# One stretch a round for the 64-wide matmuls of a two-layer graph network

## The chip, the cores and the metric

The kernel runs on one core of a Trainium2 chip. Its time is the device time of one execution in microseconds (us). The core has a matrix engine (PE, TensorE), whose results go to PSUM, eight banks of 128 partitions by 512 fp32; a vector engine (DVE), an activation engine (ACT) and GpSimd (POOL)[...]; and SP, which here issues nearly all DMA transfers. Each engine has its own queue of instructions and takes them in order; semaphores tie the queues together.

## What is computed

Sixty-four graphs of 256 nodes with 512 features pass through two layers, all in fp32. Layer 0 is attention with eight heads of 64 and a gate, layer 1 graph attention. Cut to what matters:

```python
h = relu(layernorm(x))                        # layer 0
q, k, v = h @ Wq.T, h @ Wk.T, h @ Wv.T         # 8 heads of 64
scores = where(adj != 0, q @ k.T / 8, -inf)    # per head
c = softmax(scores) @ v
gate = sigmoid(concat([c, h]) @ Wg.T + bg)
x = x + gate * h + (1 - gate) * c
h = relu(layernorm(x))                        # layer 1
Wh = h @ W
e = leaky_relu(Wh @ a1 + (Wh @ a2).T, 0.2)     # masked by adj
x = x + elu(softmax(e) @ Wh)
```

## The kernel before, in words

**Tiles.** A graph's 256 nodes are two tiles of 128 (NT = 2), its 512 features four chunks of 128 (HC = 4). Everything stays fp32. A matmul of fp32 stands in the trace as two instructions.

**Products by Strassen.** The four large products, qk (q and k together), v, z (the gate) and wh, are done in seven steps instead of eight (`strassen`, L158). Steps 1 and 2 write PSUM bank a, steps 6, 7 and 4 bank b, steps 5 and 3 bank c. Between them partial sums are taken out: u1, u2, u3, and the four blocks of the result, c00, c01, c10, c11. u1 and c00 are copies on ACT (L187), the others additions on DVE (L185). u2 and u3 read bank b between steps 6, 7 and 4, and c11 reads bank c between steps 5 and 3, so PE may not go on in a bank before DVE has read it. The order in which steps and sums are issued is written out by hand. The sums of input blocks that Strassen needs are made on POOL (`token_sums`, L146, instructions L152 to L155).

**Attention.** Heads come in two halves of four; a half has two pairs jj, a pair two heads i. `a_scores` (L328) multiplies 64 rows of q with 64 rows of k (L338, shape 64\*128: the two heads of a pair use the upper and lower half of the array at once) into four PSUM tiles `ps`, one for each head. `a_max` (L349) has DVE add the mask and find the row's extreme (L353), `a_exp` (L358) is the exponential on ACT (L362), `a_scale` (L367) multiplies by the reciprocal of the sum on POOL (L374), `a_turn` (L376) transposes 32x32 blocks on DVE (L383). `a_send` writes the blocks to DRAM and `a_fetch` (L401) reads them back in the transposed order, both on SP's queue. `a_weigh` (L407) multiplies with v (L415, shape 128\*64, again two at a time) into the tile `pc`, and `a_evac` copies that to cT on ACT (L425). All other matmuls use the whole array, shape 128\*128.

**The gate and layer 1.** z is the gate's product, `g_tanh` is on ACT, `g_mix` (L460) on DVE. The result is transposed and sent through DRAM (y), added to x (`g_residual`), normalised, transposed and sent again (h1), and multiplied into wh. `g_edges` transposes the edge column on PE (L554, tile `pe`), `g_logits`, `g_leaky`, `g_exp` are layer 1's attention, `g_out` its product (L613, tile `po`), and `g_neg`, `g_pos`, `g_elu`, `g_add` the final function and sum.

**Rounds.** `emit_round(i)` (L648) issues one round, for five graphs at once: p = i + 1 is projected (qk, v), i is in attention, q = i - 1 in its gate, r = i - 2 in layer 1's attention, o = i - 3 is stored. There is no scheduler: under a manual schedule each engine's queue has the order of the calls in `emit_round`. A round's matmuls before the change, in order: z(q), wh(r), scores of i's second half, weighings of its first half, `pe`, qk(p), v(p), output tile 0 of r, scores of p's first half, weighings of i's second half, output tile 1.

**The next h.** A graph's first normalised h goes the same way a round earlier: normalised on ACT (L213), transposed by blocks on DVE (`p_turn`, L239), sent to DRAM (`there_h`) and fetched (`p_fetch`, L269, tile `hT_l`) by SP, whose queue takes all these transfers in the order of the calls; `p_sums` makes its Strassen sums on POOL, and qk needs both.

**Buffers.** PSUM has one tile each for banks a, b and c and five tiles for everything else (tag w). In SBUF the pools that the change touches are qk (3 tiles) and e (4 tiles, for scores, for their blocks, and for the transposed blocks alike).

Of the kernel before, what the change touches and what calls it, by code (L numbers as in the profile page):

```python
# [22 lines left out]
def kernel(  # L23
# [44 lines left out]
    def pool(name, bufs, **kw):  # L68
# [2 lines left out]
    const = pool("const", 1)  # L71
    st = pool("st", 3)
    sb = {tag: pool(tag, bufs) for tag, bufs in {
        "x": 5, "adj": 1, "mask": 4, "hT": 3, "S": 3, "qk": 3, "v": 2, "wh": 1, "e": 4,
        "cT": 1, "z": 2, "h": 1, "tmp": 5, "U": 3,
    }.items()}
    ps = {tag: pool(f"ps_{tag}", bufs, space=bass.MemoryType.PSUM) for tag, bufs in {
# [250 lines left out]
    def a_scores(g, half):  # L328
        s = graphs[g]
        qk = s["qk"][half]  # L330
        psc = {}
        for jj in range(2):
            for i in range(2):
                psc[jj, i] = ps["w"].tile([P, NT, N], F32, tag="t", name=f"ps_{g}_{half}_{jj}_{i}")
            for t in range(NT):
                for i in range(2):
                    r = i * DK
                    nc.tensor.matmul(  # L338
                        psc[jj, i][:, t, :], qk[r:r + DK, 0, jj, t * P:(t + 1) * P], qk[r:r + DK, 1, jj, :],
                        start=True, stop=True,  # L340
                    )
        s["ps", half] = psc
        for jj in range(2):
            s["e", half, jj] = sb["e"].tile([P, 2, NT, N], F32, tag="t", name=f"e_{g}_{half}_{jj}")
        s["low", half], s["sums", half], s["rec", half] = (
            st.tile([P, 2, 2, NT], F32, tag=tag, name=f"{tag}_{g}_{half}") for tag in ("low", "sums", "rec")
        )
# [16 lines left out]
                accum_out=s["sums", half][:, jj, i, t:t + 1],  # L364
            )

    def a_scale(g, half, jj):  # L367
        s = graphs[g]
        rec = s["rec", half][:, jj]
        nc.vector.reciprocal(rec, s["sums", half][:, jj])  # L370
        for i in range(2):
            for t in range(NT):
                e = s["e", half, jj][:, i, t, :]
                nc.gpsimd.tensor_scalar(e, e, rec[:, i, t:t + 1], 1.0, ALU.mult, ALU.mult)  # L374

    def a_turn(g, half, jj, i):  # L376

# [29 lines left out]
    def a_weigh(g, half):  # L407
        s = graphs[g]
        eT = [s.pop(("eT", half, jj)) for jj in range(2)]
        pc = s["pc"] = ps["w"].tile([P, 2, N], F32, tag="t", name=f"pc_{g}_{half}")  # L410
        for jj in range(2):
            for kc in range(NT):
                for i in range(2):
                    hd = 4 * half + 2 * jj + i
                    nc.tensor.matmul(  # L415
                        pc[i * DK:(i + 1) * DK, jj, :].rearrange("p (t a c) -> p t a c", t=NT, c=32),
                        s["v"][:, kc, hd * DK:(hd + 1) * DK], eT[jj][:, i, kc],
                        start=(kc == 0), stop=(kc == NT - 1),
                    )
# [79 lines left out]
    def g_residual(g):  # L499
        s = graphs[g]  # L500
        for t in range(NT):
            x = s["x"][:, t, :]
            if g >= LAST:
                nc.vector.tensor_tensor(x, x, s["py"][t], ALU.add)
            else:
                x = x.rearrange("p (j i c) -> p j i c", i=4, c=32)
                nc.vector.tensor_tensor(x, x, s["yT"][:, :, t].rearrange("p i j c -> p j i c"), ALU.add)

    def g_stats(g, t):
        norm_stats(graphs[g], t, f"l1_{g}")  # L510
# [137 lines left out]
    def emit_round(i):  # L648


        p, q, r, o = i + 1, i - 1, i - 2, i - 3

        def do(fn, g, *args):
            if 0 <= g < B:
                fn(g, *args)

        def run(fn, g, steps):
            if 0 <= g < B:
                if (fn, g) not in products:
                    products[fn, g] = fn(g), set()  # L660
                product, done = products[fn, g]
                for step in steps.split():
                    if step not in done:
                        product(step)
                        done.add(step)


        run(g_gate, q, "1")
        do(g_neg, o, 1)
        do(p_turn, p)  # L670
        do(p_send, p)
        do(a_scale, i, 0, 0)
        do(a_exp, i, 0, 1, 0)
        do(a_exp, i, 0, 1, 1)
        run(g_gate, q, "u1 6 u2 5")
        do(a_scale, i, 0, 1)
        do(a_turn, i, 0, 0, 0)
        do(a_turn, i, 0, 0, 1)
        do(a_send, i, 0, 0)
        do(g_pos, o, 1)  # L680
        do(g_sums_h, r)
        run(g_gate, q, "7")
        do(a_turn, i, 0, 1, 0)
        do(a_turn, i, 0, 1, 1)
        do(a_send, i, 0, 1)
        do(p_fetch, p)
        do(a_fetch, i, 0, 0)
        do(g_diff, q)
        run(g_gate, q, "u3 c11")
        do(p_mask, p)  # L690
        chore(chores, 2)
        do(g_elu, o, 1)
        run(g_gate, q, "2 c00 4 c10")
        do(g_tanh, q, 0)
        do(a_fetch, i, 0, 1)
        run(g_gate, q, "3 c01")
        do(g_mix, q, 0, True)

        run(g_wh, r, "1 u1")
        do(g_tanh, q, 1)  # L700
        do(g_mix, q, 0, False)
        run(g_wh, r, "6 u2 5")
        do(g_mix, q, 1, True)
        run(g_wh, r, "7 u3")
        do(g_mix, q, 1, False)
        chore(chores, 2)
        run(g_wh, r, "c11 2 c00")
        do(p_sums, p)
        do(g_turn, q)
        do(g_send, q)  # L710
        run(g_wh, r, "4 c10 3 c01")
        do(a_scores, i, 1)
        if i > 0:
            do(a_weigh, i, 0)
        do(a_max, i, 1, 0)
        do(g_add, o, 0)
        do(g_add, o, 1)
        do(g_store, o)
        do(a_exp, i, 1, 0, 0)
        do(a_exp, i, 1, 0, 1)  # L720
        do(a_max, i, 1, 1)
        if i > 0:
            do(a_evac, i, 0)
        do(g_fetch, q)
        do(g_edges, r)
        do(a_exp, i, 1, 1, 0)
        do(g_logits, r)
        do(a_scale, i, 1, 0)
        do(g_leaky, r)
        if i == -1:  # L730
            chore(weight_sums("q"), 4)
            chore(weight_sums("k"), 4)
        run(p_qk, p, "1")
        do(a_exp, i, 1, 1, 1)
        do(g_exp, r)
        do(a_scale, i, 1, 1)
        if i == 0:
            run(p_qk, p, "u1 6 u2 5 7 u3 c11 2 c00 4 c10")
            a_weigh(i, 0)
            a_evac(i, 0)  # L740
        do(a_turn, i, 1, 0, 0)
        do(a_turn, i, 1, 0, 1)
        do(a_send, i, 1, 0)
        do(load_graph, p + 1)
        if i == -1:
            for key in ("gh", "gc", "1"):
                load_weight(key, nc.sync)
            load_small()
            chores.extend(weight_sums("gh") + weight_sums("gc"))
            chores.append(lambda: nc.vector.tensor_scalar_mul(hbg, hbg, 0.5))  # L750
            chores.extend(edge_columns() + weight_sums("1"))
        run(p_qk, p, "u1 6 u2 5")
        do(g_turn_e, r)
        do(g_send_e, r)
        do(g_rec, r)
        do(a_turn, i, 1, 1, 0)
        do(a_turn, i, 1, 1, 1)
        do(a_send, i, 1, 1)
        run(p_qk, p, "7 u3 c11")
        chore(chores, 1)  # L760
        do(a_fetch, i, 1, 0)
        do(g_fetch_e, r)
        do(a_fetch, i, 1, 1)
        do(g_residual, q)
        run(p_qk, p, "2 c00")
        do(g_stats, q, 0)
        run(p_qk, p, "4 c10")
        chore(chores, 1)
        do(g_stats, q, 1)
        do(g_root, q)  # L770
        run(p_qk, p, "3 c01")
        chore(chores, 1)
        if i == -1:
            chore(weight_sums("v"), 4)
        run(p_v, p, "1 u1")
        do(g_bias, q)
        do(g_norm, q)
        run(p_v, p, "6 u2 5")
        if q < LAST:
            do(g_turn_h, q)  # L780
            do(g_send_h, q)
        run(p_v, p, "7 u3 c11 2 c00")
        chore(chores, 1)
        do(p_stats, p + 1, 0)
        run(p_v, p, "4 c10")
        chore(chores, 1)
        do(p_stats, p + 1, 1)
        do(p_root, p + 1)
        run(p_v, p, "3 c01")
        chore(chores, 1)  # L790
        do(p_bias, p + 1)
# [63 lines left out]
```

## Time and profile before

| | |
|---|---|
| median of 3 runs | 3233.6 us (3232.44 to 3236.47) |
| profiled execution, its own time | 3231.35 us |
| its span from first to last instruction | 3229.6 us |
| granted clock of PE | 0.992 |
| busy: PE, DVE, POOL, ACT | 3169.3, 2526.9, 1716.3, 1304.5 us |
| DMA | 590.66 MB, mean 183 GB/s |

The profile is one execution on the chip. A busy time is the union of an engine's instructions; matmuls are pipelined and their recorded times overlap, so the distance between the starts of two matmuls tells more than how long each is. A line of the timeline has start, duration, engine, line of the kernel, operation, the tile written and the tiles read, shapes and a count; a bracket at its end tells how long the engine stood idle before it and what released it. `PEld` is the loading of weights into the array.

### The profile page before, as it was taken

What the parts mean: (1) busy time and instruction counts of PE and PEld (TensorE: products, weight loads), DVE (VectorE), ACT (ScalarE), POOL (GpSimd) and SP (SyncE); (2) the same over time, 40 slices, a digit from 0 to 9 for tenths busy, and PEclk for the clock granted to TensorE, in tenths of its full rate; (3) what the DMA queues carried; (4) which work ended last, traced back from release to release, by engine and by line L of the source; (5) the groups of instructions that cost most, each with busy time, mean ns of one, the idle gap of its engine ahead of it and who ended that gap; (6) DMA issues with size and microseconds to landing.
All of it is one profiled execution on the core that took longest, in us unless ns stands there. A gap on an engine that the chain in (4) does not pass through costs nothing.

```text
span 3229.6 us, 67257 instructions
## 1 busy us (share of the span) xinstructions
PE 3169.3 (98%) x22716; PEld 2703.0 (84%) x22716; DVE 2526.9 (78%) x6366; ACT 1304.5 (40%) x3720; POOL 1716.3 (53%) x2439
## 2 busy tenths in 40 slices
PE   7999999999999999999999999999999999999996
PEld 6888888888888888888888888888888888888884
DVE  6778778788787787787787787887887877877874
ACT  2343443443443443444434334434434444344342
POOL 2555654655655545546556546556455455465453
PEclk9999999999999999999999999999999999999998
DMA  5677677777777777777776777777777777777751
GB/s 163 172 186 192 185 189 196 183 183 197 184 183 202 178 189 193 188 188 187 188 193 181 190 195 184 181 200 184 182 196 186 188 193 187 188 188 189 193 148 46
DMA packets 1103399, 590.66 MB, mean 183 GB/s; under 512 B 685776, under 2 KB 1029328, under 8 KB 1103056
## 3 DMA queue, kind: packets, MB, share of 16 engines
q1 hardware_dynamic: 1102000, 585.32, 69.2%
q8 instruction: 181, 2.97, 0.4%
q14 instruction: 162, 1.33, 0.1%
q10 hardware_dynamic: 1056, 1.05, 0.1%
HBM read 304.88 MB, written 281.28 MB: 181 GB/s over the span
## 4 chain that ended last, share of the span: by engine, by line
PE 94%; DMA 1%; issue 1%; DVE 1%; POOL 1%; SPq 1%; ACT 1%; POOLq 0%; DVEq 0%; ACTq 0%
PE pmb_qk L174 11%; PE pmb_z L174 10%; PE pc L415 7%; PE ps L338 7%; PE po L613 7%; PE pma_qk L174 7%; PE pmc_qk L174 7%; PE pmc_z L174 7%; PE pma_z L174 7%; PE pmb_v L174 5%; PE pmb_wh L174 5%; PE pmc_wh L174 4%; PE pmc_v L174 3%; PE pma_v L174 3%; PE pma_wh L174 3%
## 5 line engine op out<-in xcount | busy, mean ns | idle before, releaser
L374 POOL TENSOR_SCALAR e<-e,rec 128x256 f32<-128x256 f32 x1024 | 496.5, 508 | 305.8 <-DVE rec L370 235.2
L362 ACT ACTIVATE e<-e,low 128x256 f32<-128x256 f32 x1024 | 506.2, 497 | 219.5 <-DVE low L353 219.5
L204 POOL TENSOR_TENSOR rs_l<-ve_l,mhalf 128x2 f32<-128x2 f32 x128 | 89.1, 696 | 885.6 <-DVE ve_l L200 885.6
L353 DVE CUSTOM_DVE_ANT_0 e<-ps,mask 128x256 f32<-128x256 f32 x1024 | 363.1, 420 | 35.9 <-PE ps L338 32.4
L383 DVE STREAM_TRANSPOSE eb<-e 128x512 f32<-128x512 f32 x512 | 345.0, 694 | 29.9 <-POOL e L374 25.8
L415 PE MATMUL pc<-eT,v 128*64 128x256 f32 x2048 | 252.4, 388 | 10.0 <-DMA eT<-there_e 10.0
L338 PEld LDWEIGHTS ps<-qk 64*128 64x128 f32 x2048 | 188.6, 187 | 86.7 <-issue 68.0
L338 PE MATMUL ps<-qk 64*128 64x256 f32 x2048 | 258.2, 391 | 0.4 <-DVE low L353 0.4
L613 PE MATMUL po<-wh,egT 128*128 128x512 f32 x512 | 254.4, 620 | 2.7 <-ACT egT L596 2.1
L415 PEld LDWEIGHTS pc<-eT,v 128*64 128x64 f32 x2048 | 136.8, 137 | 110.5 <-issue 32.9
L213 ACT ACTIVATE h_l<-x,nb_l,rs_l 128x512 f32<-128x512 f32 x256 | 194.6, 809 | 10.0 <-DVE nb_l L208 9.6
L362 ACT ACTIVATION_READ_ACCUMULATOR e<-e,low 128x1 f32 x1024 | 193.4, 189 | 0.0
L625 ACT ACTIVATE pos<-po,rec 128x512 f32<-128x512 f32 x128 | 87.8, 686 | 258.0 <-DVE neg L620 258.0
L453 POOL TENSOR_TENSOR d<-hT_l,cT 128x512 f32<-128x512 f32 x128 | 186.1, 1474 | 0.0
L196 DVE BATCH_NORM_STATS2 bs_l<-x 128x6 f32<-128x512 f32 x256 | 175.0, 684 | 5.3 <-DMA x<-in_x_dram 5.3
L152 POOL TENSOR_TENSOR S_l<-hT_l 128x256 f32<-128x256 f32 x128 | 101.6, 794 | 141.7 <-DMA hT_l<-there_h 114.8
L613 PEld LDWEIGHTS po<-wh,egT 128*128 128x128 f32 x512 | 93.9, 195 | 98.0 <-issue 68.3
L635 POOL TENSOR_TENSOR x<-x,pos 128x512 f32<-128x512 f32 x128 | 160.9, 1277 | 15.5 <-DVE pos L631 15.5
L187 ACT COPY qk<-pma_qk 128x512 f32<-128x512 f32 x64 | 37.5, 586 | 323.7 <-PE pma_qk L174 323.7
L458 ACT ACTIVATE z<-z,hbg 128x256 f32<-128x256 f32 x256 | 116.2, 502 | 124.6 <-DVE z L185 124.6
L239 DVE STREAM_TRANSPOSE h_l<-h_l 128x512 f32<-128x512 f32 x248 | 161.1, 687 | 2.5 <-ACT h_l L213 2.4
L620 DVE TENSOR_SCALAR neg<-po,rec 128x512 f32<-128x512 f32 x128 | 95.3, 745 | 82.0 <-PE po L613 82.0
(145 smaller groups left out, 8059.9 us busy)
## 6 DMA issues: line engine op xcount, KB each, us to landing
there_e<-eb SPq DMA_DIRECT2D x256, 512.0 KB, 4.1
eT<-there_e SPq DMA_DIRECT2D x1024, 128.0 KB, 3.5
there_h<-h_l SPq DMA_DIRECT2D x496, 128.0 KB, 3.3
hT_l<-there_h SPq DMA_DIRECT2D x496, 128.0 KB, 3.2
x<-in_x_dram SPq DMA_DIRECT2D x64, 512.0 KB, 4.9
out_dram<-x SPq DMA_DIRECT2D x64, 512.0 KB, 3.2
there_y<-y SPq DMA_DIRECT2D x62, 512.0 KB, 2.6
yT<-there_y SPq DMA_DIRECT2D x248, 128.0 KB, 3.3
```

Source lines behind the costliest of these rows:

```text
L174: nc.tensor.matmul(bank[key][(slice(None), *cols)], lhsT, rhs, start=first and i == 0, stop=last and i == len(todo) - 1, skip_group_check= ...
L196: nc.vector.bn_stats(bs, s["x"][:, t, :])
L213: nc.scalar.activation(h[:, t, :], s["x"][:, t, :], AF.Relu, bias=s["nb"][:, t:t + 1], scale=s["rs"][:, t:t + 1])
L239: nc.vector.transpose(h[:, t, :], h[:, t, :])
L338: nc.tensor.matmul(psc[jj, i][:, t, :], qk[r:r + DK, 0, jj, t * P:(t + 1) * P], qk[r:r + DK, 1, jj, :], start=True, stop=True,)
L353: nc.vector.tensor_tensor_reduce(s["e", half, jj][:, i, t, :], s["ps", half][jj, i][:, t, :], s["mask"][:, t, :], -SCALE, HUGE, ALU.add, A ...
L362: nc.scalar.activation(e, e, AF.Exp, bias=s["low", half][:, jj, i, t:t + 1], scale=-1.0, accum_out=s["sums", half][:, jj, i, t:t + 1],)
L374: nc.gpsimd.tensor_scalar(e, e, rec[:, i, t:t + 1], 1.0, ALU.mult, ALU.mult)
L383: nc.vector.transpose(s["eb", half, jj][:, :, 4 * i:4 * i + 4, :].rearrange("p b n c -> p n b c"), e)
L415: nc.tensor.matmul(pc[i * DK:(i + 1) * DK, jj, :].rearrange("p (t a c) -> p t a c", t=NT, c=32), s["v"][:, kc, hd * DK:(hd + 1) * DK], eT[ ...
L453: nc.gpsimd.tensor_tensor(d, s["hT"][:, :, js, :], s["cT"][:, :, js, :], ALU.subtract)
L613: nc.tensor.matmul(pm, s["egT"][:, t, kc, :], s["wh"][:, kc, :, :HH], start=(kc == 0), stop=(kc == NT - 1))
```

## The change

- Scores and weighings stand together. After v(p), the weighings of both halves of i are done, then the scores of both halves of p, then both output tiles of r. The scores of the second half are thus a part of the round before.
- Scores of both halves are eight PSUM tiles, and five of tag w are too few: three of them take the products' banks, one tile of the first half bank c, two of the second half banks b and c.
- qk gets two tiles, e five.
- `a_scale` can scale on ACT; in each round the fourth group (second half, second pair) is scaled there, the other three on POOL. The form of the instruction on POOL is the same before and after.
- All four groups of a graph are scaled, transposed and sent during the gate of the round. Before, the second half's were so during qk.
- In wh, c11 is taken out before the second half's last mix. `pe` stands after step 1 of qk. The residual and statistics of the two tiles are issued apart; final functions (`g_neg` to `g_add`) are moved, and so is the transposition of the next h (`p_turn`), from the next round into this one's end.
- The last three rounds (`tail`) have an order of their own.

```diff
@@ -71,7 +71,7 @@
     const = pool("const", 1)
     st = pool("st", 3)
     sb = {tag: pool(tag, bufs) for tag, bufs in {
-        "x": 5, "adj": 1, "mask": 4, "hT": 3, "S": 3, "qk": 3, "v": 2, "wh": 1, "e": 4,
+        "x": 5, "adj": 1, "mask": 4, "hT": 3, "S": 3, "qk": 2, "v": 2, "wh": 1, "e": 5,
         "cT": 1, "z": 2, "h": 1, "tmp": 5, "U": 3,
     }.items()}
     ps = {tag: pool(f"ps_{tag}", bufs, space=bass.MemoryType.PSUM) for tag, bufs in {
@@ -328,10 +328,10 @@
     def a_scores(g, half):
         s = graphs[g]
         qk = s["qk"][half]
-        psc = {}
+        psc, where = {}, {(0, 0, 0): "mc", (1, 1, 0): "mb", (1, 1, 1): "mc"}
         for jj in range(2):
             for i in range(2):
-                psc[jj, i] = ps["w"].tile([P, NT, N], F32, tag="t", name=f"ps_{g}_{half}_{jj}_{i}")
+                psc[jj, i] = ps[where.get((half, jj, i), "w")].tile([P, NT, N], F32, tag="t", name=f"ps_{g}_{half}_{jj}_{i}")
             for t in range(NT):
                 for i in range(2):
                     r = i * DK
@@ -364,14 +364,17 @@
                 accum_out=s["sums", half][:, jj, i, t:t + 1],
             )
 
-    def a_scale(g, half, jj):
+    def a_scale(g, half, jj, on_act=False):
         s = graphs[g]
         rec = s["rec", half][:, jj]
         nc.vector.reciprocal(rec, s["sums", half][:, jj])
         for i in range(2):
             for t in range(NT):
                 e = s["e", half, jj][:, i, t, :]
-                nc.gpsimd.tensor_scalar(e, e, rec[:, i, t:t + 1], 1.0, ALU.mult, ALU.mult)
+                if on_act:
+                    nc.scalar.activation(e, e, AF.Copy, scale=rec[:, i, t:t + 1])
+                else:
+                    nc.gpsimd.tensor_scalar(e, e, rec[:, i, t:t + 1], 1.0, ALU.mult, ALU.mult)
 
     def a_turn(g, half, jj, i):
 
...
@@ -664,36 +666,46 @@
                         product(step)
                         done.add(step)
 
+        tail = i >= B - 1
 
         run(g_gate, q, "1")
         do(g_neg, o, 1)
-        do(p_turn, p)
         do(p_send, p)
-        do(a_scale, i, 0, 0)
-        do(a_exp, i, 0, 1, 0)
-        do(a_exp, i, 0, 1, 1)
-        run(g_gate, q, "u1 6 u2 5")
+        do(g_pos, o, 0)
+        run(g_gate, q, "u1")
         do(a_scale, i, 0, 1)
         do(a_turn, i, 0, 0, 0)
         do(a_turn, i, 0, 0, 1)
         do(a_send, i, 0, 0)
-        do(g_pos, o, 1)
-        do(g_sums_h, r)
-        run(g_gate, q, "7")
+        do(a_exp, i, 1, 0, 0)
+        do(a_exp, i, 1, 0, 1)
         do(a_turn, i, 0, 1, 0)
+        run(g_gate, q, "6 u2")
         do(a_turn, i, 0, 1, 1)
         do(a_send, i, 0, 1)
+        do(g_sums_h, r)
+        do(g_elu, o, 0)
+        run(g_gate, q, "5")
+        do(a_scale, i, 1, 0)
+        do(g_pos, o, 1)
+        run(g_gate, q, "7 u3 c11")
+        do(a_exp, i, 1, 1, 0)
+        do(a_exp, i, 1, 1, 1)
+        do(a_scale, i, 1, 1, True)
+        do(a_turn, i, 1, 0, 0)
+        do(a_turn, i, 1, 0, 1)
+        do(a_send, i, 1, 0)
+        do(a_turn, i, 1, 1, 0)
+        do(g_diff, q)
+        run(g_gate, q, "2 c00 4 c10")
+        do(g_tanh, q, 0)
+        do(a_turn, i, 1, 1, 1)
+        do(a_send, i, 1, 1)
         do(p_fetch, p)
-        do(a_fetch, i, 0, 0)
-        do(g_diff, q)
-        run(g_gate, q, "u3 c11")
         do(p_mask, p)
         chore(chores, 2)
-        do(g_elu, o, 1)
-        run(g_gate, q, "2 c00 4 c10")
-        do(g_tanh, q, 0)
-        do(a_fetch, i, 0, 1)
         run(g_gate, q, "3 c01")
+        do(a_fetch, i, 0, 0)
         do(g_mix, q, 0, True)
 
         run(g_wh, r, "1 u1")
@@ -701,46 +713,35 @@
         do(g_mix, q, 0, False)
         run(g_wh, r, "6 u2 5")
         do(g_mix, q, 1, True)
-        run(g_wh, r, "7 u3")
+        run(g_wh, r, "7 u3 c11")
         do(g_mix, q, 1, False)
         chore(chores, 2)
-        run(g_wh, r, "c11 2 c00")
+        run(g_wh, r, "2 c00 4")
         do(p_sums, p)
         do(g_turn, q)
         do(g_send, q)
-        run(g_wh, r, "4 c10 3 c01")
-        do(a_scores, i, 1)
-        if i > 0:
-            do(a_weigh, i, 0)
-        do(a_max, i, 1, 0)
-        do(g_add, o, 0)
-        do(g_add, o, 1)
-        do(g_store, o)
-        do(a_exp, i, 1, 0, 0)
-        do(a_exp, i, 1, 0, 1)
-        do(a_max, i, 1, 1)
-        if i > 0:
-            do(a_evac, i, 0)
+        do(a_fetch, i, 0, 1)
+        run(g_wh, r, "c10 3 c01")
         do(g_fetch, q)
-        do(g_edges, r)
-        do(a_exp, i, 1, 1, 0)
-        do(g_logits, r)
-        do(a_scale, i, 1, 0)
-        do(g_leaky, r)
+        do(a_fetch, i, 1, 0)
+
         if i == -1:
             chore(weight_sums("q"), 4)
             chore(weight_sums("k"), 4)
-        run(p_qk, p, "1")
-        do(a_exp, i, 1, 1, 1)
+        run(p_qk, p, "1 u1")
+        do(g_edges, r)
+        do(g_logits, r)
+        do(g_leaky, r)
+        run(p_qk, p, "6 u2 5")
+        do(g_elu, o, 1)
+        do(g_add, o, 1)
+        do(g_add, o, 0)
+        do(g_store, o)
         do(g_exp, r)
-        do(a_scale, i, 1, 1)
-        if i == 0:
-            run(p_qk, p, "u1 6 u2 5 7 u3 c11 2 c00 4 c10")
-            a_weigh(i, 0)
-            a_evac(i, 0)
-        do(a_turn, i, 1, 0, 0)
-        do(a_turn, i, 1, 0, 1)
-        do(a_send, i, 1, 0)
+        do(g_turn_e, r)
+        do(g_send_e, r)
+        do(g_rec, r)
+        run(p_qk, p, "7 u3 c11 2 c00")
         do(load_graph, p + 1)
         if i == -1:
             for key in ("gh", "gc", "1"):
@@ -749,64 +750,66 @@
             chores.extend(weight_sums("gh") + weight_sums("gc"))
             chores.append(lambda: nc.vector.tensor_scalar_mul(hbg, hbg, 0.5))
             chores.extend(edge_columns() + weight_sums("1"))
-        run(p_qk, p, "u1 6 u2 5")
-        do(g_turn_e, r)
-        do(g_send_e, r)
-        do(g_rec, r)
-        do(a_turn, i, 1, 1, 0)
-        do(a_turn, i, 1, 1, 1)
-        do(a_send, i, 1, 1)
-        run(p_qk, p, "7 u3 c11")
         chore(chores, 1)
-        do(a_fetch, i, 1, 0)
+        do(a_fetch, i, 1, 1)
         do(g_fetch_e, r)
-        do(a_fetch, i, 1, 1)
-        do(g_residual, q)
-        run(p_qk, p, "2 c00")
+        do(g_residual, q, 0)
+        run(p_qk, p, "4 c10")
+        do(g_residual, q, 1)
+        chore(chores, 1)
+        run(p_qk, p, "3 c01")
+        chore(chores, 1)
         do(g_stats, q, 0)
-        run(p_qk, p, "4 c10")
-        chore(chores, 1)
+        if i == -1:
+            chore(weight_sums("v"), 4)
+        run(p_v, p, "1 u1 6 u2")
         do(g_stats, q, 1)
         do(g_root, q)
-        run(p_qk, p, "3 c01")
-        chore(chores, 1)
-        if i == -1:
-            chore(weight_sums("v"), 4)
-        run(p_v, p, "1 u1")
+        run(p_v, p, "5 7 u3 c11")
         do(g_bias, q)
         do(g_norm, q)
-        run(p_v, p, "6 u2 5")
-        if q < LAST:
+        run(p_v, p, "2 c00")
+        chore(chores, 1)
+        if not tail:
             do(g_turn_h, q)
             do(g_send_h, q)
-        run(p_v, p, "7 u3 c11 2 c00")
+        run(p_v, p, "4 c10")
+        chore(chores, 1)
+        run(p_v, p, "3 c01")
         chore(chores, 1)
         do(p_stats, p + 1, 0)
-        run(p_v, p, "4 c10")
-        chore(chores, 1)
         do(p_stats, p + 1, 1)
         do(p_root, p + 1)
-        run(p_v, p, "3 c01")
-        chore(chores, 1)
+        do(g_sums, i)
+        if tail:
+            do(g_out, r, 0)
+            do(g_out, r, 1)
+            do(g_turn_h, q)
+
+        do(a_weigh, i, 0)
+        do(a_evac, i, 0)
+        do(a_weigh, i, 1)
+        do(a_evac, i, 1)
+        do(a_sums, i)
+        do(a_scores, p, 0)
+        do(a_scores, p, 1)
+        if not tail:
+            do(g_out, r, 0)
+            do(g_out, r, 1)
+        do(a_max, p, 0, 0)
         do(p_bias, p + 1)
-        do(g_out, r, 0)
-        do(g_neg, r, 0)
-        do(g_pos, r, 0)
-        do(a_scores, p, 0)
-        do(a_weigh, i, 1)
-        do(g_out, r, 1)
-        if q >= LAST:
-            do(g_turn_h, q)
-        do(a_max, p, 0, 0)
         do(a_exp, p, 0, 0, 0)
         do(a_max, p, 0, 1)
-        do(a_evac, i, 1)
-        do(g_sums, i)
-        do(a_sums, i)
+        do(a_exp, p, 0, 0, 1)
+        do(p_norm, p + 1)
+        do(a_max, p, 1, 0)
+        do(a_max, p, 1, 1)
         do(g_fetch_h, q)
-        do(p_norm, p + 1)
-        do(a_exp, p, 0, 0, 1)
-        do(g_elu, r, 0)
+        do(a_scale, p, 0, 0)
+        do(a_exp, p, 0, 1, 0)
+        do(a_exp, p, 0, 1, 1)
+        do(g_neg, r, 0)
+        do(p_turn, p + 1)
 
     with tc.manual_schedule(engines={getattr(mybir.EngineType, e) for e in ("PE", "SP", "Pool", "DVE", "Activation")}):
         load_graph(0)
```

More of the change, by code (lines that the diff above doesn't have):

```diff
@@ L497, in g_fetch, with g_residual @@
             fetch(s["yT"].rearrange("p i t j c -> p i (t j c)"), s.pop("there"))
-    def g_residual(g):
+    def g_residual(g, t):
         s = graphs[g]
[L501 to L507, printed above, removed]
+        x = s["x"][:, t, :]
+        if g >= LAST:
+            nc.vector.tensor_tensor(x, x, s["py"][t], ALU.add)
+        else:
+            x = x.rearrange("p (j i c) -> p j i c", i=4, c=32)
+            nc.vector.tensor_tensor(x, x, s["yT"][:, :, t].rearrange("p i j c -> p j i c"), ALU.add)
     def g_stats(g, t):
```

## The prediction

> **What bounds the kernel now.** I read the page first: the busy times and the chain that ended last, then the order of matmuls in one steady round, then the waits.
>
> ```profile
> PE 3169.3 (98%) x22716; PEld 2703.0 (84%) x22716; DVE 2526.9 (78%) x6366; ACT 1304.5 (40%) x3720; POOL 1716.3 (53%) x2439
> ...
> PE 94%; DMA 1%; issue 1%; DVE 1%; POOL 1%; SPq 1%; ACT 1%; POOLq 0%; DVEq 0%; ACTq 0%
> ```
>
> PE sets the end: only time between PE's matmuls can be won. A busy PE isn't a PE at its peak, so I looked at the distances of starts. The timeline of PE, one round (start, duration, line, output and inputs, count):
>
> ```profile
> 1471.09 1.03 PE L174 MATMUL pmb_wh<-w_t,hT_l 128*128 128x257 f32 x4
> 1472.15 1.11 PE L174 MATMUL pmc_wh<-w_sb,S_l 128*128 128x257 f32 x4
> 1473.19 2.00 PE L338 MATMUL ps<-qk 64*128 64x256 f32 x16
> 1475.12 1.95 PE L415 MATMUL pc<-eT,v 128*64 128x256 f32 x16
> 1476.99 0.43 PE L554 MATMUL pe<-ident,wh 128*128 128x128 f32 x2
> 1477.26 1.06 PE L174 MATMUL pma_qk<-hT_l,wq_sb 128*128 128x128 f32 x8
> ...
> 1494.09 1.03 PE L174 MATMUL pmb_v<-wv_t,hT_l 128*128 128x256 f32 x4
> 1494.95 1.03 PE L174 MATMUL pmc_v<-wv_sb,S_l 128*128 128x256 f32 x4
> 1495.82 1.88 PE L613 MATMUL po<-wh,egT 128*128 128x512 f32 x4
> 1497.63 2.00 PE L338 MATMUL ps<-qk 64*128 64x256 f32 x16
> ```
>
> Undisturbed, four matmuls of 256 columns take 0.86 (1494.09 to 1494.95): 0.216 each. Sixteen scores or weighings run two at a time, 8 x 0.216 = 1.73; scores take 1.93, weighings 1.88. Four output matmuls of 512 should take 1.72; before scores they take 1.81 (1495.82 to 1497.63). The excess sits where array shape 128*128, 64*128 or 128*64 changes. In the single records each change costs 0.09 between the last matmul of one shape and the first of the next, and a first load that nothing hides: 0.10 for scores, 0.05 for weighings, 0.10 for outputs, 0.05 for the two edge transposes. The round has two chains full, scores, weighings, full, that is six changes: 6 x 0.09 + 2 x 0.10 + 2 x 0.05 + 0.10 + 0.05 = 0.99.
>
> A second bubble: step 4 of the wh product takes 1.06 (median 1.00) instead of 0.87, and the first load of step 3 shows (0.08). Step 3 writes bank c, which DVE must have read for c11, and c11 is queued behind a mix:
>
> ```profile
> 1470.76 0.91 DVE L468 SCALAR_TENSOR_TENSOR z<-d,cT 128x512 f32<-128x512 f32 x1
> ...
> 1471.60 0.41 DVE L185 TENSOR_TENSOR wh<-pmc_wh,u_wh 128x257 f32<-128x257 f32 x1
> ```
>
> That is 0.13 + 0.08 = 0.21 in a median round. From the gate's first block at 128.50 to that at 3121.77 lie 61 rounds: mean 49.07, median 49.00. Outside are a head and a tail in which PE does wait.
>
> **What the Trainium skill says.** "TensorEngine Tiling (Array Packing)", Key Properties: "Mode switching requires drain". The trace agrees, with 0.09 a change. "TensorE: Matmul & The Clock Gate", What overlaps and what doesn't (under The mechanism): a weight load hides under a running matmul only in another row group; the trace shows 0.05 to 0.10 exposed at each change, though it also hides loads of one shape behind one another. "ScalarE: Activation LUTs", Table sets: cheap functions, copy among them, are in every set, so scaling by Copy on ACT should load no table; this trace has one load for relu, exp, tanh and copy. "GPSIMD Engine Reference", Specifications: GpSimd shares its SBUF interfaces with VectorE instructions that read two SBUF inputs; here the mix of POOL (L453) takes 1.47 against 1.26 when DVE leaves it alone, and DVE's elu 1.21 against 0.69.
>
> **The change part by part.**
> 1. One stretch. Full, weighings of both halves, scores of both halves of the next graph, outputs: three changes. 3 x 0.09 + 0.05 + 0.10 + 0.10 = 0.52, so 0.99 - 0.52 = 0.47 less a round.
> 2. c11 is moved ahead of the mix: 0.21 less. The number of matmuls is the same. Round: 49.00 - 0.47 - 0.21 = 48.32; with the present scatter (mean over median, 0.07) 48.39.
> 3. Eight score banks in five w slots, one b and two times c. Bank c comes back for the last scores when DVE has read the first two tiles: first scores start 7.2 before the gate, DVE begins 1.16 later (1473.19 to 1474.35), two passes of 0.35 end 5.3 before it, PE wants c at 4.5 before. b and c are wanted by gate steps 6 and 5, at +1.8 and +3.6; DVE's sixteen passes (16 x 0.347 = 5.6, and a bias) end at -0.3. Outputs want slots of passes long done. Free, cover 0.8 and more; where DVE starts late by more, PE waits one for one.
> 4. Scales. The form on POOL (L374) is the same text before and after. One group of four moves to ACT: POOL loses 4 x 0.485 = 1.9 a round, ACT gains, estimated at the skill's price in "ScalarE: Activation LUTs", What ACT_TABLE_LOAD costs (186 + 0.833 x 256 + 93 = 492 ns, 93 of it overlapped), 1.6; the trace has 0.50 for such tiles (L458), so 2.0 at most. ACT is 40% busy. Free.
> 5. Orders. All four groups are now scaled, transposed (L383) and sent during the gate, half of it formerly during the qk product. DVE between gate step 1 and step 3's end is the tight place. Times from the gate's start, with the profile's distances: passes end -0.3; reciprocal, neg 0.67, two h transposes 1.22, neg 0.67, reciprocal: 2.5. POOL gets that 0.3 later, scales 1.85 to 4.7, does the four h1 sums (4 x 0.69, and 0.3 of contention with elu) to 7.8, scales the third group to 9.7. DVE meanwhile: three transposes to 4.5, u2 4.9 (step 7 wants it at 5.4), transpose, elu, u3 at 7.4 (PE), c11. Then two transposes behind POOL to 10.4, one to 11.1, c10, the last to 12.1, mask 12.8. The gate's c01 can start at 12.77, when step 3 is out (before: 1515.96 less 1503.19, the same 12.77). After it come two mixes and u2 of wh, which step 7 of wh waits for: PE already loses 0.05 there. So any lateness of that chain goes to PE one for one. On means instead of distances it is 0.6 to 0.8 late; with no contention 0. I take 0.10, range 0 to 0.8.
> 6. DMA. SP is passed in order, so the fetch of the next h (four DMAs) now stands behind the fourth send, at 12.4 instead of 9. From first issue to all landed it takes 5.2 (p90 5.9, longest 7.2): 17.6 to 18.3, and qk step 1 wants it at 18.7; the first sums, 1.7 on POOL, are wanted by step 6 at 20.5. Cover about 1; without it PE waits one for one. The four eT fetches land by 38 and weighings begin at 37.5 and 39.4 (only the last fetch comes so late, for the second half). The y store shares four DRAM buffers with the sends and waits for the first eT fetch, to 20.5; its fetch then lands near 29, before the residual's neighbours matter to PE (30.4).
> 7. Smaller pools and e's fifth buffer: qk's two halves die together after the stretch, so two suffice; e needs four live score tiles and one more. Free.
>
> Sum a round: 48.39 + 0.10, I take 48.47: 0.60 less, x 61 = 37.
>
> Head: PE waits between 77 and 106 for weighings' data (1.83, 0.72, 3.81) and scores (3.9). With weights after a whole qk and v these go, but the second graph's h then comes about 3 late, and its sums stand behind three scales instead of two. I take 5 (0 to 10).
>
> Tail: before, the last scores at 3142.74 start a chain of exp, scale, send and fetch to the weighing at 3159.89:
>
> ```profile
> 3145.80 1.95 PE L415 MATMUL pc<-eT,v 128*64 128x256 f32 x16
> 3147.67 0.43 PE L554 MATMUL pe<-ident,wh 128*128 128x128 f32 x2
> 3151.23 1.39 PE L594 MATMUL ptr<-ident,eg 128*128 128x128 f32 x4 [3.13 <-ACT eg L576]
> 3153.36 3.78 PE L613 MATMUL po<-wh,egT 128*128 128x512 f32 x4 [0.73 <-ACT egT L596]
> 3159.89 1.46 PE L415 MATMUL pc<-eT,v 128*64 128x256 f32 x8 [2.76 <-DMA eT<-there_e]
> ```
>
> The last gate starts 46.6 after the one before it (3168.37 less 3121.77). Now those scores are done a stretch earlier; what remains is mix, residual, statistics, norm, transposes and two weighings, some 36. Less 1 to 2 for the last elu's, now one behind the other: 9 (4 to 12).
>
> 37 + 5 + 9 = 51 off the profiled execution's 3231.35 (its span 3229.6): 3180. The median of the runs is 2.25 above it: 3183.
>
> **The rivals.**
> A, forecast: the changes of shape pay, the gate chain is at most 0.3 late: 3165 to 3200. Chance 0.60.
> B: DVE and POOL become the bound in the gate; c01 is 0.5 to 0.9 late every round, PE waits at wh step 7. For it: DVE's waits on POOL's scale, and 11.6 of DVE work in 12.8. Against: the distances above, POOL's lost 1.9. 3183 + 61 x (0.3 to 0.7) = 3201 to 3226. Chance 0.22.
> C, slower: the fetch of h behind the fourth send. Four sends of 0.5 MB stand in the queues before it within 8 us, formerly two. If it lands at 20.5 instead of 18, PE waits 1.8 at qk step 1: 3183 + 61 x 1.8 = 3293. It ends slower than before once it takes over 7.2 from its issue (18.7 + 0.85 against 12.4), the longest of 124 now. For it: POOL's sums wait for this DMA already (114.8 us in all). Chance 0.11.
> D: drains are not saved because what follows a merge waits for banks or ACT's copies anyway; only head and tail pay: 3215 to 3235. Chance 0.07.
>
> **How the numbers follow.** About 0.2% (6.5 us) is what a measurement can tell from no change: faster is under 3227, slower over 3240. A and B are faster, most of D too; C is slower, some of D the same: 0.86, 0.03, 0.11. Range: best case 48.32 a round and 22 at the ends, 3164; upper, B's end, 3228; C and a part of D stay outside. A alone is 3165 to 3200.
>
> **What would show it.** Three changes of shape a round instead of six, blocks of 32 scores at about 3.6; wh step 4 at 0.87; gate starts 48.5 apart. B shows as a gap before wh step 7 released by DVE; C as a gap before qk step 1 by DMA; D as waits inside the stretch. A table load of 1.28 (L213) in each round would make all this wrong.

## The result and the profile after

The kernel after takes 3190.8 us (median of 4 runs, 3185.72 to 3191.47), the kernel before, run beside it, 3233.9: ratio 0.986, 95% interval 0.9845 to 0.988. The forecast was 3183, 3165 to 3200 for its likeliest case. Run again in another comparison, beside the later experiments, it took 3193.6, ratio 0.987 (0.9856 to 0.9883).

The page of the profiled execution (3185.72 us, span 3183.9), busy times and the chain that ended last:

```profile
PE 3125.0 (98%) x22716; PEld 2723.9 (86%) x22716; DVE 2467.8 (78%) x6366; ACT 1413.6 (44%) x3976; POOL 1506.3 (47%) x2183
...
PE 90%; DVE 4%; POOL 2%; DMA 2%; issue 1%; SPq 1%; ACT 0%; DVEq 0%; POOLq 0%; ACTq 0%
```

The same 22,716 matmuls in 44 us less of busy PE. ACT won 109 us: the fourth group of scales. POOL lost 210: 144 in its scales, which are 256 fewer, and the rest in its differences (1.47 to 1.27 on the mean) and sums, which are shorter. The timeline of PE, one round, in the columns used before:

```profile
1506.09 1.03 PE L174 MATMUL pmc_wh<-w_sb,S_l 128*128 128x257 f32 x4
1506.95 1.05 PE L174 MATMUL pma_qk<-hT_l,wq_sb 128*128 128x128 f32 x8
...
1524.86 1.03 PE L174 MATMUL pmc_v<-wv_sb,S_l 128*128 128x256 f32 x4
1525.81 3.68 PE L418 MATMUL pc<-eT,v 128*64 128x256 f32 x32
1529.42 3.72 PE L338 MATMUL ps<-qk 64*128 64x256 f32 x32
1533.08 3.71 PE L615 MATMUL po<-wh,egT 128*128 128x512 f32 x8
1536.62 1.05 PE L174 MATMUL pma_z<-hT_l,wgh_sb 128*128 128x128 f32 x8
```

Three changes of shape are left (1525.81, 1529.42, 1533.08), and no wait stands between the blocks: 3.61, 3.66, 3.54 from start to start. Step 3 of wh (1506.09 to 1506.95) takes 0.86. On DVE, c11 of wh now stands ahead of the last mix:

```profile
1553.31 0.43 DVE L185 TENSOR_TENSOR wh<-pmc_wh,u_wh 128x257 f32<-128x257 f32 x1
1553.65 0.68 DVE L471 SCALAR_TENSOR_TENSOR z<-d,cT 128x512 f32<-128x512 f32 x1
```

At the end, the last weighings and the last gate stand together, without a wait for a fetch; the last gate starts 36.5 after the one before it (46.6 before):

```profile
3119.93 3.67 PE L418 MATMUL pc<-eT,v 128*64 128x256 f32 x32
3123.54 1.16 PE L174 MATMUL pma_z<-hT_l,wgh_sb 128*128 128x128 f32 x8
```

Three of PE's waits (us in total, times, longest):

```profile
PE pma_qk L174 <- DMA hT_l<-there_h: 10.1, 9, 6.0
PE ptr L596 <- ACT eg L578: 9.6, 4, 3.2
PE pmb_qk L174 <- POOL S_l L153: 4.0, 1, 4.0
```

The first is the change's own: qk waits for the next h, 6.0 at once for the third graph's, and up to 1.0 in some steady rounds. The second was there before (9.5). The third is qk of the second graph, in the first round, which waits for its sums on POOL; before, it waited 0.5 for them and 4.8 more at its step 7, which the profile puts down to POOL's scales.

Where the 45.7 us between the two spans came from, by the starts of the gates: 61 steady rounds, 49.07 to 48.52 on the mean (median 49.01 to 48.32): 33.8. Up to the second gate, 128.50 to 127.62: 0.9. From the gate before the last to the end, 107.8 to 96.9: 10.9. The second profile of the same kernel (span 3188.9) has 32.1, -0.7 and 9.3: the rounds agree within 2 us, and the program's start and end vary by 1.6 us each between these two executions.

### The profile page after: what moved, and what is told of

It is laid out like the page before. It is cut to its first block, busy times and chain, and to the rows that moved or that the text cites. A ratio compares the mean times of both kernels' runs of the same rounds, so it can differ in the third digit from the quotient of the medians.

```text
span 3183.9 us, 66670 instructions
## 1 busy us (share of the span) xinstructions
PE 3125.0 (98%) x22716; PEld 2723.9 (86%) x22716; DVE 2467.8 (78%) x6366; ACT 1413.6 (44%) x3976; POOL 1506.3 (47%) x2183
## 4 chain that ended last, share of the span: by engine, by line
PE 90%; DVE 4%; POOL 2%; DMA 2%; issue 1%; SPq 1%; ACT 0%; DVEq 0%; POOLq 0%; ACTq 0%
PE pmb_qk L174 11%; PE pmb_z L174 9%; PE pc L418 7%; PE pma_qk L174 7%; PE pmc_qk L174 7%; PE ps L338 6%; PE po L615 6%; PE pma_z L174 6%; PE pmc_z L174 6%; PE pmb_v L174 5%; PE pmb_wh L174 5%; PE pma_v L174 3%; PE pmc_v L174 3%; PE pmc_wh L174 3%; PE pma_wh L174 3%; DVE e L353 1%
## 5 line engine op out<-in xcount | busy, mean ns | idle before, releaser
L377 POOL TENSOR_SCALAR e<-e,rec 128x256 f32<-128x256 f32 x768 | 352.7, 477 | 148.8 <-DVE rec L370 100.4
L386 DVE STREAM_TRANSPOSE eb<-e 128x512 f32<-128x512 f32 x512 | 351.8, 696 | 76.7 <-POOL e L377 63.4
L152 POOL TENSOR_TENSOR S_l<-hT_l 128x256 f32<-128x256 f32 x128 | 93.4, 730 | 395.9 <-DMA hT_l<-there_h 361.9
L615 PE MATMUL po<-wh,egT 128*128 128x512 f32 x512 | 242.5, 617 | 2.1 <-ACT egT L598 2.1
L338 PE MATMUL ps<-qk 64*128 64x256 f32 x2048 | 238.9, 383 | 0.6 <-DVE v L185 0.6
L418 PE MATMUL pc<-eT,v 128*64 128x256 f32 x2048 | 235.9, 382 | 0.1
L456 POOL TENSOR_TENSOR d<-hT_l,cT 128x512 f32<-128x512 f32 x128 | 160.5, 1274 | 0.0
L428 ACT COPY cT<-pc 128x512 f32<-128x512 f32 x128 | 74.9, 585 | 184.5 <-PE pc L418 184.5
L174 PEld LDWEIGHTS pma_z<-hT_l,wgh_sb 128*128 128x128 f32 x1024 | 129.2, 192 | 30.4 <-issue 30.4
L174 PE MATMUL pma_qk<-hT_l,wq_sb 128*128 128x128 f32 x1024 | 139.6, 280 | 11.9 <-DMA hT_l<-there_h 10.1
```

The lines of the kernel that those rows point to most:

```text
L174: nc.tensor.matmul(bank[key][(slice(None), *cols)], lhsT, rhs, start=first and i == 0, stop=last and i == len(todo) - 1, skip_group_check= ...
L338: nc.tensor.matmul(psc[jj, i][:, t, :], qk[r:r + DK, 0, jj, t * P:(t + 1) * P], qk[r:r + DK, 1, jj, :], start=True, stop=True,)
L386: nc.vector.transpose(s["eb", half, jj][:, :, 4 * i:4 * i + 4, :].rearrange("p b n c -> p n b c"), e)
L418: nc.tensor.matmul(pc[i * DK:(i + 1) * DK, jj, :].rearrange("p (t a c) -> p t a c", t=NT, c=32), s["v"][:, kc, hd * DK:(hd + 1) * DK], eT[ ...
L456: nc.gpsimd.tensor_tensor(d, s["hT"][:, :, js, :], s["cT"][:, :, js, :], ALU.subtract)
L615: nc.tensor.matmul(pm, s["egT"][:, t, kc, :], s["wh"][:, kc, :, :HH], start=(kc == 0), stop=(kc == NT - 1))
```

## The experiments

None of these kernels leaves out work. Each ran beside the kernel before, and kernels of different experiments are compared by their ratios to it. "Mean round" is the mean over the 61 rounds between the second gate and the last but one.

**c11 alone, in the kernel before.**

```diff
-        run(g_wh, r, "7 u3")
+        run(g_wh, r, "7 u3 c11")
         do(g_mix, q, 1, False)
         chore(chores, 2)
-        run(g_wh, r, "c11 2 c00")
+        run(g_wh, r, "2 c00")
```

> The kernel before with one edit: in wh, c11 is taken out of bank c ahead of the last mix. If the second part of the sum holds (0.13 at wh step 4 and 0.08 at step 3 in a median round, plus the longer waits of some rounds at the same place, 14 us in all), this alone gives 10 to 15 us: 3219 to 3224, ratio 0.9955 to 0.997. Rival: the mix that is now late, or the next sum, puts PE in the same wait elsewhere, and nothing is gained: within 3 us of before.

3220.1 us beside 3239.2 for before: ratio 0.9943 (0.9931 to 0.9956), 14 to 22 less, where 10 to 15 were expected. One round of it on PE:

```profile
1464.35 1.03 PE L174 MATMUL pmb_wh<-w_t,hT_l 128*128 128x257 f32 x4
1465.21 1.03 PE L174 MATMUL pmc_wh<-w_sb,S_l 128*128 128x257 f32 x4
1466.17 2.00 PE L338 MATMUL ps<-qk 64*128 64x256 f32 x16
```

From start to start, wh steps 4 and 3 take 0.868 and 0.960 in the median round (before 0.999 and 1.036): 0.21 less. On the mean the two steps win 14.2 over the rounds, of which some 1.7 come back later in the round, most at the last step of v: 12.5 are left in the trace. The rival falls: most of the wait did not move on, and the second part of the forecast's sum is shown by itself. Why the times differ by a few us more than the traces do stays open.

**Two more changes of shape, in the kernel after.**

```diff
         do(a_scores, p, 0)
+        if not tail:
+            do(g_out, r, 0)
         do(a_scores, p, 1)
         if not tail:
-            do(g_out, r, 0)
             do(g_out, r, 1)
```

> The kernel after, with one output tile put between the scores of the first and of the second half: two more changes of the array's shape a round, and nothing else moved. If a change costs what the single records of before show (0.09 each, and a first load of 0.10 for scores and 0.10 for outputs), a round is 0.38 longer, about 23 us in all: 3212 to 3217 where the kernel after is 3190.8. Rival D (what follows a merge waits for banks or for copies anyway): no more than 3 us.

3221.0 us, ratio 0.9952 (0.9939 to 0.9966): 27 to 29 us above the two measurements of after, a little more than the 23 expected; the mean round is 0.50 longer. One round of it on PE:

```profile
1545.70 2.00 PE L338 MATMUL ps<-qk 64*128 64x256 f32 x16
1547.63 1.99 PE L615 MATMUL po<-wh,egT 128*128 128x512 f32 x4
1549.55 2.00 PE L338 MATMUL ps<-qk 64*128 64x256 f32 x16
1551.47 1.99 PE L615 MATMUL po<-wh,egT 128*128 128x512 f32 x4
```

From start to start: scores 1.93 and 1.92, outputs 1.92 and 1.83, together 7.60, against 7.20 for the two blocks of after. That is 0.20 for a change and its first load, where 0.19 was reckoned. The other 0.10 is waits: gate step 7 is 0.03 later (the last scores reach DVE 1.9 later, so its passes end later), and weighings and qk step 1 wait for their DMAs a little more. Rival D falls: the merge is worth its drains.

**The fourth group back on POOL, in the kernel after.**

```diff
-        do(a_scale, i, 1, 1, True)
+        do(a_scale, i, 1, 1)
```

> The kernel after, with the fourth group scaled on POOL as the other three. POOL's third group ended at +10.0 after the gate's start and ACT's fourth at +10.1; the fourth on POOL would end near +11.9, the last two transposes, mask and c01 of the gate come 0.2 to 0.5 later. If that chain has no cover (theory: any lateness goes to PE one for one), 12 to 30 us more than the kernel after, as a gap ahead of wh step 7. Rival: DVE's queue had waited for something else there, the cover is over 0.5, and the time stays within 3 us.

3281.0 us, ratio 1.0131 (1.0117 to 1.0144): 84 to 87 us above after, slower than before, and far above the 12 to 30 expected. PE's waits name the place:

```profile
PE pmb_wh L174 <- DVE u_wh L185: 37.7, 61, 0.6
PE pmc_wh L174 <- DVE z L185: 29.9, 57, 0.6
```

wh step 5 now waits too: it writes bank c, which the gate's c01 (z on DVE) must have read. In one round whose gate starts at 1583.23, DVE:

```profile
1594.72 0.69 DVE L386 STREAM_TRANSPOSE eb<-e 128x512 f32<-128x512 f32 x1
1595.34 2.07 DVE L222 TENSOR_SCALAR mask<-adj 128x512 bf16<-128x512 int32 x1
1597.33 0.41 DVE L185 TENSOR_TENSOR z<-pmc_z,u_z 128x256 f32<-128x256 f32 x1
```

and POOL:

```profile
1591.00 3.65 POOL L377 TENSOR_SCALAR e<-e,rec 128x256 f32<-128x256 f32 x8
1594.62 2.50 POOL L456 TENSOR_TENSOR d<-hT_l,cT 128x512 f32<-128x512 f32 x2
```

The last transpose ends no later than in after (+12.2 here, +12.5 in the round that starts at 1536.62; in the median 0.1 later). But POOL's two differences, behind eight scales instead of four, now run to 1597.12 instead of ending as the mask begins, and the mask, 0.39 in after, takes 2.07. In all 62 rounds that have a mask it is long, and it ends 0.28 after the end of POOL's second difference each time. c01 is thus 1.4 late, not 0.2 to 0.5. The Trainium skill has this as an exclusive lock between the two engines, not a shared bandwidth ("Trainium Architecture — The Big Picture", What this means for kernel authors). It also says that a DVE instruction with a single source and its destination in SBUF can take a mode that uses both ports ("VectorE: DVE Perf Modes", What auto-detection actually checks); the mask is one, and 0.39 for 512 elements, where a mix of as many takes 0.68, agrees. The trace of before had it already: there the mask took 0.77 in the median round, and in 59 of 62 it ended 0.28 after one of POOL's instructions, as here after a sum:

```profile
1511.15 0.73 POOL L154 TENSOR_TENSOR S_l<-hT_l 128x256 f32<-128x256 f32 x1
1511.40 0.76 DVE L222 TENSOR_SCALAR mask<-adj 128x512 bf16<-128x512 int32 x1
```

The forecast counted only DVE's instructions with two inputs in SBUF as held up by POOL.

**The same, with the mask out of the way.**

```diff
-        do(p_mask, p)
         chore(chores, 2)
         run(g_gate, q, "3 c01")
...
         do(g_mix, q, 1, False)
+        do(p_mask, p)
```

> All four groups on POOL as in the run before (3281), and the mask of the next graph, which stands in DVE's queue ahead of the gate's c01, moved behind the last mix. There the mask took 2.07 instead of 0.39 and ended 0.28 after POOL's second difference in nearly every round. Theory: the mask can't run while POOL works on two tiles of SBUF, and this alone held c01, wh step 5 and step 7 back: with the mask away c01 waits for step 3 only, and the time is that of the kernel after, 3188 to 3200. Rival: POOL with four groups is itself late (its fourth group ends 1.9 later and the transposes behind it): 3205 to 3220 (0.2 to 0.5 a round), or still above 3260 if the difference is what is waited for.

3240.6 us, ratio 1.0016 (1.0009 to 1.0023): some 40 of the 84 to 87 us come back, 47 stay. wh step 5 no longer waits (0.87), step 7 does (its turn comes 1.80 after step 5 starts, instead of 0.87). The theory was half right: with the mask gone, the first mix, which reads two tiles of SBUF, runs into the same differences. DVE, in the round whose gate starts at 1562.1:

```profile
1574.86 0.42 DVE L185 TENSOR_TENSOR z<-pmc_z,u_z 128x256 f32<-128x256 f32 x1
1575.23 1.75 DVE L469 SCALAR_TENSOR_TENSOR d<-z,d 128x512 f32<-128x512 f32 x1
```

Its own input d was ready: no idle time stands before it. c01, which reads one of its two inputs from PSUM, ran in 0.42 under the same difference. In 61 of the 64 gates the mix ends 0.55 after the second difference does. That the difference as such, wherever it stands, costs these 47 us is argued from the durations; moving it on POOL was not tried.

**The fetch of the next h earlier.**

```diff
         do(a_send, i, 0, 1)
+        do(p_fetch, p)
...
         do(a_send, i, 1, 1)
-        do(p_fetch, p)
```

> The kernel after, with the fetch of the next h put between the second and the third send, where SP's queue has some 4 us with nothing to issue. It is issued about 5 us earlier. If qk step 1 waits for this DMA (8 us in the steady rounds, and 2 to 4 in the head, where the third graph's h was late), 7 to 12 us less than the kernel after: 3179 to 3184. Rival: the next in line (POOL's sums behind the two differences, or the fourth send, now later) takes its place, within 3 us of after.

3183.6 us, ratio 0.9831 (0.9817 to 0.9844): 10 to 13 us less than after by the ratios. The h landed at +14.1 after the gate's start (median) instead of +18.4, and qk step 1, at +18.6, waits in no steady round. In the trace the mean round is only 0.07 to 0.10 shorter, some 5 us, because the weighings now waited for the last fetch of eT, which stands on SP behind the load of the next x: in ten rounds they took 0.2 to 1.1 longer, 5 us in all (0.9 and 2.6 us in the two traces of after).

**The fetch later.**

```diff
-        do(p_fetch, p)
...
         do(a_fetch, i, 0, 0)
+        do(p_fetch, p)
```

> The kernel after, with the fetch of the next h put behind the first fetch of eT, which takes SP 2.0 to issue: 2.1 later. If that fetch has no cover left (rival C's mechanism: PE waits one for one at qk step 1), 1.9 to 2.2 more in each of 61 rounds, 115 to 135 us: 3305 to 3325, slower than before. If it had the cover of about 1 that the forecast gave it: 60 to 75 us, 3250 to 3265. If POOL's sums or something else covers it: the time of after.

3361.8 us, ratio 1.0401 (1.0385 to 1.0416), 168 us above after.

```profile
PE pma_qk L174 <- DMA hT_l<-there_h: 147.1, 62, 7.8
```

The fetch was issued 2.2 later (+15.2 instead of +13.0) and landed 2.5 later (20.83 instead of 18.35); qk step 1 started 2.4 later. Behind the wait the first eight matmuls of qk step 1 took 0.97 instead of 0.89 in 46 of the 61 rounds, and 1.36 to 1.84 in the other 15. In exactly these 15 the granted clock of PE falls to 0.5 for 3.4 us, near the end of the wait. Two stretches of 3 us behind a wait, one of each kind (from and to, length, busy time and instructions of PE, granted clock, DMA):

```profile
2203.40:2206.40 3.00, 3.00 (x14) 0.50 1.01 218
2409.30:2412.30 3.00, 3.00 (x27) 1.00 0.83 217
```

The first follows a wait of 2.3, the second the longest of the steady rounds, 3.2: the length of the wait does not decide it here. Together 2.7 a round, over the 1.9 to 2.2 expected: 2.3 of wait and 0.4 of slower matmuls. Hardly any cover was left in after, and rival C's mechanism is real: 2.2 on SP's queue put the kernel 4% behind before.

**Two fetches and sums.** The early fetch; the last fetch of eT ahead of the loads of the next graph; and the first round's sums ahead of the scales:

```diff
+        if i == 0:
+            p_sums(p)
         run(g_gate, q, "1")
...
-        do(p_sums, p)
+        if i != 0:
+            do(p_sums, p)
...
         do(a_fetch, i, 1, 0)
+        do(a_fetch, i, 1, 1)
...
         do(load_graph, p + 1)
...
-        do(a_fetch, i, 1, 1)
         do(g_fetch_e, r)
```

> The kernel after with three edits of order: the fetch of the next h between the second and third send (3183.6 where done alone); the last fetch of eT ahead of the loads of the next graph, whose x waits for the store of an older one (PE waited 5.8 us for that fetch in the steady rounds of the run with the early fetch); and in the first round the sums of h on POOL ahead of the scales (the second graph's qk waited 5.6 us for them). Theory: the second edit 4 to 6 less, the third 3 to 5 less: 3172 to 3178. Rival: the second and third only move the wait, to layer 1's fetch and to the scales that are now later: 3181 to 3186.

3182.4 us, ratio 0.9838 (0.9825 to 0.9851): no better than the early fetch alone. The second edit did what was expected of it: no weighing waits any more (3.604 in every steady round). The third moved the wait: qk of the second graph waits 5.7 for u2 on DVE, which stands behind transposes of blocks that POOL scales later, instead of 4.0 for the sums.

**Without the third edit,** that is the early fetch and:

```diff
         do(a_fetch, i, 1, 0)
+        do(a_fetch, i, 1, 1)
...
-        do(a_fetch, i, 1, 1)
         do(g_fetch_e, r)
```

> The kernel after with the fetch of the next h between the second and third send and the last fetch of eT ahead of the loads of the next graph; the third edit of the run before this one (sums ahead of scales in the first round) is left out. In that run the second graph's qk took 36.56 from its first matmul to the gate, against 33.25 with the early fetch alone: the wait of 5.6 for the sums had become one of 5.8 at step 5, and later ones. If so, 3 us less than that run's 3182.4: 3177 to 3181. Rival: the start of the program differs from run to run by as much, and the sums ahead cost nothing: 3181 to 3184.

3178.3 us, ratio 0.9817 (0.9804 to 0.9831): the fastest measured, 15 to 17 us below after by the ratios, though its interval and that of the early fetch alone overlap. Mean round 48.37, median 48.30.

**And the mask behind the last mix,** in the kernel just above:

```diff
-        do(p_mask, p)
         chore(chores, 2)
         run(g_gate, q, "3 c01")
...
         do(g_mix, q, 1, False)
+        do(p_mask, p)
```

> The same, and the mask behind the last mix instead of ahead of the gate's c01. c01 and the mixes come 0.4 earlier where DVE is what they wait for; wh step 7 waited for u2 by 0.05 on the mean in the rounds of the run with the early fetches. Theory: 2 to 4 us less than without (3174 to 3178). Rival: POOL's sums of the next h, which the early fetch lets begin at the same time as the mixes, take the place of the mask in holding DVE up, and nothing is gained.

3184.3 us, ratio 0.9838 (0.9824 to 0.9851): 6 us more. Theory wrong, rival right: in 19 rounds the mask ran into POOL's sums and took up to 0.95, and the edge transposes on PE, behind the last sums of wh in DVE's queue, waited for it (5.3 us). Ahead of c01, the mask begins as the differences end.

**The kernel after, unchanged,** was run beside three of these; its numbers stand in the section on the result.

> The kernel after, unchanged, beside the three that follow, so that they can be compared on one chip. 0.9845 to 0.988 of before, as in its first comparison; no theory asks for another value.

## Why the prediction was right

**Changes of shape: right.** Forecast 0.47 a round. The blocks that the merge touches take 13.34 before (with wh step 3 as in the run with c11 alone, 0.96) and 12.85 after: 0.49.

**c11: right.** Forecast 0.21, measured 0.21 alone; in the whole, wh step 4 takes the same 0.868. Median round 48.32, forecast 48.32.

**Banks: right.** In no steady round did a score block wait for a bank (3.654 to 3.655 throughout). What the forecast did not say is that in the first two gates no outputs stand between the scores and the gate yet: there step 6 waited for bank b, 1.0 and 1.15.

**Scales: right in size, and weightier than said.** On ACT one takes 0.497 (forecast 0.49 to 0.50), hidden, and the whole program still has one table load. "Free" was the price of moving it; what it buys was not told: with it left on POOL, the change would have lost to before.

**The gate's chain (rival B): 0.10 was set, 0.00 came.** c01 starts at +12.71 in the median, as before (+12.70), and wh steps 5 and 7 take 0.868 and 0.921 in the median round, as before (0.868 and 0.919). The contention that the forecast allowed for didn't fall on this chain: DVE's mask and mixes began as POOL's differences ended (mask at +12.41, end of the second difference at +12.47). The forecast had not placed the two against each other, so this was luck. The run with four groups on POOL shows how near the edge this is: 1.9 us more of POOL make B cost 1.45 a round, not the 0.3 to 0.7 reckoned: the rival counted that results come late, and not that POOL's differences hold up DVE's instructions.

**DMA: the cover was mis-sized.** Forecast: issued at +12.4, landed by 17.6 to 18.3, wanted at 18.7, cover about 1. Measured medians: issued at +13.0 (the last transpose ended at +12.5, not 12.1), 5.34 long, landed at 18.35, wanted at 18.64: cover 0.3, and waits in the rounds in which it took longer, 0.14 on the mean. Rival C thus came in a mild form, and by chance filled the 0.10 that B left: mean round 48.52, forecast 48.47.

**The head: this step failed in size.** 5 forecast, 0.9 and -0.7 measured. The waits for weighings' data, 6.4 in all, went, as said, and the first gate came at 78.6 and 80.0 instead of 83.7. (The 3.9 for scores that the forecast lists beside them is no other wait: no scores wait there, and 3.9 is what passes between the end of the scores at 96.86 and the weighings, the 3.81 once more.) What was under-counted is what came in their place. The third graph's h, whose fetch stands behind four sends there too, came late:

```profile
99.62 2.05 PE L174 MATMUL pma_qk<-hT_l,wq_sb 128*128 128x128 f32 x8 [6.00 <-DMA hT_l<-there_h]
```

Between the gate and this product lie 6.2, and another 2.1 went in slow matmuls behind the wait, in a stretch whose granted clock is 0.5 (97.0 to 103.9): together 8.3, as much as the waits for weighings' data had cost with the slow matmuls behind them (8.1). The second graph's qk waited 4.0 for its sums behind three groups of scales, with slow matmuls 5.6 in all. The forecast had about 3 for the second graph's h and its sums, and nothing for the third graph's. With the early fetch the wait for this h was 1.9 instead of 6.0, but 2.9 of waits for POOL and DVE came behind it; from the second graph's first matmul to the second gate that kernel took 80.5, the kernel after 82.2 and 83.1, the kernel before 81.4. With the sums first as well it was 83.4. What the head is bound by in the end stays open.

**The tail: right.** 9 forecast, 10.9 and 9.3 measured; the last gate starts 36.5 after the one before it, where some 36 was forecast. (The order of the tail holds from round 63 on, which is four rounds, not three.)

Sum: 51 forecast, 45.7 and 40.7 by the two profiles; the 5 to 10 that are missing are the head (4 and 6) and the rounds (3 and 5, the waits for h in the main). Three of the forecast's sums are off by small amounts that change no reading: 48.39 and 0.10 give 48.49, not 48.47; the best case of 3164 lacks the 2.25 that the other times have; and rival B's own sum ends at 3226, not 3228.

## What to carry to other kernels

Before a step is moved in a queue that is taken in order, find the transfer that is behind it and work out its cover from the trace; here 2.2 us more in one queue cost 5%, and two lines of order on it won another half a per cent. A change of the array's shape had the same price each time here (0.14 to 0.20 with its load, by shape), which can be read off once and counted. And where two engines exclude one another, it isn't the load of either that counts but which instructions meet: look for durations that are several times the usual.

## What was not expected of the hardware

- POOL's differences and sums hold up some of DVE's instructions to their end, and one input from SBUF can be enough: the mask (one input) took 0.39 beside nothing, 0.77 behind one of POOL's sums, 2.07 behind two differences of 1.25 that followed at once, always ending 0.28 after POOL's instruction. A mix (two inputs) took 1.75 instead of 0.68, ending 0.55 after it. An addition with one input in PSUM (0.42) was not held up, nor were the transposes of blocks, which have one input in SBUF too (0.67 to 0.71, 188 times beside a difference in the kernel after).
- A wait of PE can cost more than itself. Behind waits of 1.9 to 3.2 in the run with the late fetch, the granted clock fell to 0.5 for 3.4 us in 15 of 61 rounds, and qk step 1's first eight matmuls took up to 1.84 instead of 0.97. In the kernel after, whose waits in the steady rounds are 1.2 at most, it stayed at 1 from 103.9 to 3111. What decides in which rounds it falls stays open.
